# Two recurrent layers with routed experts on one core: GpSimd's scatters in blocks of eight that must land

## The chip, the cores and the metric

The kernel runs on one core of one Trainium2 chip. The metric is device time in microseconds (us) of one execution, as the median of several; less is better. The core has five engines that matter here: TensorE (PE), VectorE (DVE), ScalarE (ACT), GpSimd (POOL) and SyncE (SP). Each works through its own list of instructions in order and waits on semaphores for the others. SP, ACT and POOL also issue DMA transfers; all transfers of the core share 16 DMA engines.

## The reference, cut to what matters

The input is 4 sequences of 1024 tokens of 256 numbers in float32. Two layers follow, and each adds `s * silu(ffn(xn))` to `x`, where `xn` is the layer's normalised input. In layer 0 `s` is a gated recurrence, in layer 1 an attention over cosines. The part that the change touches is how tokens reach the experts of `ffn`:

```
xn = _layernorm(x, axis=-1)
topk_idx, topk_weight = _route(x, gate_weight, e_bias)      # 4 of 16 experts for each token
combine = (jax.nn.one_hot(topk_idx, E) * topk_weight[..., None]).sum(axis=1)
g = jnp.einsum('th,eih->tei', x, gate_proj)
u = jnp.einsum('th,eih->tei', x, up_proj)
act = jax.nn.silu(g) * u
expert_out = jnp.einsum('tei,ehi->teh', act, down_proj)
y = jnp.einsum('teh,te->th', expert_out, combine)
```

Layer 1 has 16 other experts, the same choice of 4, and a shared expert besides.

## The kernel before

**Routing by rows in DRAM.** The kernel computes only the chosen experts. DVE works out, for each token and each of its 4 choices, a row number in a DRAM table (`rows_in`), so that each expert's tokens stand together in tiles of 128 rows. GpSimd then scatters: one indirect DMA (L582, in `scattered`) takes 128 tokens (one column of a block of 512) and writes their 256 numbers to the 128 rows that one of the 4 choices names. A block of 512 tokens so takes 4 columns by 4 choices, 16 scatters.

**Groups.** Layer 0 has two groups of blocks (`HALVES`): three blocks (48 scatters) and five (80 scatters). Layer 1 has two groups of two sequences (`GROUPS`), four blocks or 64 scatters each. `dispatch` (L589) issues a group of layer 0; `dispatch1` (L934) one of layer 1, where GpSimd also loads each block from DRAM first (L949) and copies row information beside it (L950, L951).

**Experts.** `experts` (L596) walks over a group's rows in quads of 4 tiles: 16 and 24 quads in layer 0, 20 and 20 in layer 1. A quad is loaded three quads ahead (`load`, L621; by SP in layer 0, by ACT in layer 1), turned (L630), multiplied (L642), turned again (L659), multiplied (L667), and copied to a tile `o` by DVE (L685) and ACT (L679). There are three buffers of `xs` and three of `o`. Layer 0 stores `o` by rows (L717, ACT); layer 1 scatters it with four indirect DMAs of GpSimd per quad (L1203). Later, GpSimd gathers each token's four results of layer 0 (L724).

**What sets the order.** The program's generators are interleaved by hand with a model of time (`clock`, `pool_free`, the constants PAIR, INDIRECT and so on), and that fixes each engine's list of instructions. Waits are put in by the framework. GpSimd's DMAs take eight semaphores in turn, so that from the ninth on each scatter waits for the landing of the scatter eight before it.

Of the kernel before, what the change touches and what calls it, by code (L numbers as in the profile page):

```python
# [22 lines left out]
NS = TB // P  # L23
XB, GB, QB, OB = 8, 4, 3, 3
E, G = 16, 4
TOPK = 4
# [37 lines left out]
def two_layer_kernel(  # L64
# [18 lines left out]
    nc = tc.nc  # L83
# [488 lines left out]
    def indirect(n):  # L572

        pool_free[0] = max(pool_free[0], clock[0]) + n * INDIRECT
        return pool_free[0]

    def scattered(views, tokens, row, c0):

        indirect(len(views))
        for i, view in enumerate(views):  # L580
            s, k = divmod(i, TOPK)
            nc.gpsimd.indirect_dma_start(  # L582
                out=view,
                out_offset=bass.IndirectOffsetOnAxis(ap=row[:, c0 + s, k : k + 1], axis=0),
                in_=tokens[:, s, :],
                in_offset=None,
            )

    def dispatch(g, tokens, row):  # L589

        n = NS * TOPK
        views = dram_disjoint_views(rows_in[g], len(tokens) * n)
        for i, t in enumerate(tokens):
            scattered(views[i * n : (i + 1) * n], t, row, i * NS)

    def experts(groups, of_tiles, w_sb, we, hid, store, target=None, begin=None, end=None):  # L596

# [225 lines left out]
    def routed0(g, hs, lg):  # L823
        em, comb = yield from route(lg, len(HALVES[g]) * NS, r0b_sb, False)
        row, top, of_tile = yield from places(em, g, WE, "mm")
        dispatch(g, [hs[part] for part in HALVES[g]], row)
        with tc.issue_after(latest(mybir.EngineType.DVE)):
            w = all_of(weights_by_slot(normalized(comb), top, em, g))
        return row, w, of_tile
# [104 lines left out]
    def dispatch1(h):  # L934
        while not clearing.done:
            yield PIECE
        row, top, _ = placed1[h]
        pieces = [(b, q) for b in GROUPS[h] for q in range(NQ)]
        n = NS * TOPK
        views = dram_disjoint_views(rows_in[G1 + h], len(pieces) * n)  # L940

        tokens = {}
        for i in range(-AHEAD, len(pieces)):
            if i + AHEAD < len(pieces):
                j = i + AHEAD
                tokens[j] = t = xpool.tile([P, NS, D + INFO], F32, tag="x", name="t_half", bufs=XB)
                ts = slice(j * NS, (j + 1) * NS)
                b, q = pieces[j]
                nc.gpsimd.dma_start(out=t[:, :, 0:D], in_=block(normed, b, q))  # L949
                nc.gpsimd.tensor_copy(t[:, :, D : D + TOPK], top[:, ts, 0:TOPK])  # L950
                nc.gpsimd.tensor_copy(t[:, :, D + TOPK], result0[:, ts])  # L951
            if i >= 0:
                scattered(views[i * n : (i + 1) * n], tokens.pop(i), row, i * NS)
                while clock[0] < pool_free[0] - n * INDIRECT:
                    yield PIECE
        dispatched.add(h)
# [489 lines left out]
```

## Time and profile before

| | |
|---|---|
| three runs, median (least to most) | 1158.03 us (1157.47 to 1162.15) |
| the profiled execution's own time | 1148.62 us |
| its span, first to last instruction | 1146.9 us |
| mean granted TensorE clock in it | 0.952 |
| scatters of layer 0 (L582, from `x_half`) | 128, from 49.5 to 238.5 us, mean 1043 ns |
| scatters of layer 1 (L582, from `t_half`) | 128, from 633.4 to 806.5 us, mean 996 ns |

The profile is one execution, with times counted from its first instruction. "Busy" is time in instructions. The chain of waits follows the work that ended last back to the start. The timeline lists the instructions of an engine with the idle time in front of each and what ended it. "DMA to landing" is the time from a DMA's issue to the semaphore that tells that its data are written; for the scatters the profile has it for two of each eight, the fifth and sixth of layer 0's.

### The profile page before, as it was taken

The numbers are of one execution on the slowest core, as the hardware profiler recorded it, in microseconds if no ns is written. First come the engines' busy times: TensorE is split into PE (matmuls) and PEld (weight loads), VectorE is DVE, ScalarE is ACT, GpSimd is POOL, SyncE is SP. The second block draws the span as 40 slices with busy tenths as digits, with TensorE's granted clock in tenths as the row PEclk, the third lists the DMA queues.
The fourth block names the chain that finished last, engine by engine and source line by source line (L and its number), as shares of the span: only waits on it lengthen the run. The fifth ranks groups of instructions, "written<-read, shape, count | busy, mean of one in ns | idle before, by whom it ended". The sixth has DMA issues, their size and how long they took to land.

```text
span 1146.9 us, 16132 instructions
## 1 busy us (share of the span) xinstructions
PE 1032.5 (90%) x4928; PEld 765.6 (67%) x4928; DVE 650.2 (57%) x1963; ACT 467.2 (41%) x1030; POOL 565.0 (49%) x589
## 2 busy tenths in 40 slices
PE   5688699999889999888589999998899999999996
PEld 4255378887768788565357766765677777676665
DVE  4866953332786633167976973023633336776665
ACT  3345464444444544222143522221555555553132
POOL 1277377722760000377433777777446666776000
PEclk9868799999899999988699999999899999999999
DMA  8996569999998488977246533464545669994871
GB/s 346 396 407 253 181 204 319 328 286 274 299 302 242 134 235 243 320 189 185 84 137 243 208 122 139 140 213 139 196 163 184 188 197 353 359 337 140 273 238 37
DMA packets 118963, 264.81 MB, mean 231 GB/s; under 512 B 14177, under 2 KB 71649, under 8 KB 117601
## 3 DMA queue, kind: packets, MB, share of 16 engines
q1 hardware_dynamic: 77792, 137.18, 38.2%
q0 software_dynamic: 27264, 75.86, 19.6%
q10 hardware_dynamic: 13824, 50.75, 12.5%
q8 instruction: 43, 0.70, 0.3%
q14 instruction: 40, 0.32, 0.1%
HBM read 119.34 MB, written 144.39 MB: 230 GB/s over the span
## 4 chain that ended last, share of the span: by engine, by line
PE 65%; DVE 17%; DMA 8%; issue 4%; ACT 3%; POOL 2%; ACTq 0%; DVEq 0%; POOLq 0%
PE gu L642 14%; PE acc L667 11%; PE acc L1089 7%; PE tp L630 6%; PE gu L1136 4%; PE acc L1152 4%; PE mm L1057 4%; PE mm L1136 3%; DMA xs<-rows_in 3%; DMA r<-rows_out,row 3%; PE tp L659 3%; PE acc L296 2%; DVE x_half L1242 2%; PE mm L514 1%; DMA normed<-y 1%
## 5 line engine op out<-in xcount | busy, mean ns | idle before, releaser
L724 POOL DMA_INDIRECT r<-rows_out,row x128 | 131.4, 1027 | 240.9 <-DMA normed<-y 133.8
L642 PE MATMUL gu<-w_sb,xT 128*128 x1280 | 239.7, 331 | 0.5 <-issue 0.5
L642 PEld LDWEIGHTS gu<-w_sb,xT 128*128 128x128 f32 x1280 | 195.6, 193 | 14.6 <-issue 1.3
L1203 POOL DMA_INDIRECT results<-o,dest x160 | 159.7, 998 | 89.9 <-issue 28.2
L582 POOL DMA_INDIRECT rows_in<-x_half,row x128 | 133.5, 1043 | 101.6 <-issue 51.6
L667 PE MATMUL acc<-w_sb,hT 128*128 (+1 forms) x640 | 180.1, 397 | 2.5 <-ACT hT L661 2.4
L469 DVE SCALAR_TENSOR_TENSOR h<-sg,gu 128x256 f32<-128x256 f32 (+1 forms) x160 | 56.0, 351 | 166.9 <-ACT sg L468 166.5
L582 POOL DMA_INDIRECT rows_in<-t_half,row x128 | 127.5, 996 | 41.0 <-issue 39.0
L1089 PE MATMUL acc<-val,es 128*128 128x256 f32 x512 | 127.3, 393 | 6.3 <-ACT t L468 5.5
L634 ACT COPY xT<-tp 128x512 f32<-128x512 f32 x160 | 93.9, 587 | 91.0 <-PE tp L630 85.4
L667 PEld LDWEIGHTS acc<-w_sb,hT 128*128 128x128 f32 (+1 forms) x640 | 106.9, 189 | 30.2 <-issue 15.5
L1089 PEld LDWEIGHTS acc<-val,es 128*128 128x128 f32 x512 | 98.0, 198 | 31.1 <-issue 9.6
L630 PE MATMUL tp<-ident,xs 128*128 128x128 f32 x640 | 103.0, 285 | 11.8 <-DMA xs<-rows_in 11.8
L630 PEld LDWEIGHTS tp<-ident,xs 128*128 128x128 f32 x640 | 75.6, 144 | 46.3 <-issue 24.6
L468 ACT ACTIVATE sg<-gu 128x256 f32<-128x256 f32 (+1 forms) x160 | 52.9, 331 | 105.9 <-PE gu L642 101.1
L685 DVE COPY o<-acc 128x512 f32<-128x512 f32 x80 | 55.1, 688 | 63.4 <-PE acc L667 62.8
L659 PE MATMUL tp<-ident,h 128*128 128x128 f32 (+1 forms) x320 | 62.5, 277 | 13.4 <-DVE h L653 11.9
L1136 PE MATMUL mm<-xnT,w_sb 128*128 128x512 f32 x128 | 62.5, 611 | 11.6 <-DVE act L469 11.6
L1057 PE MATMUL mm<-projT 128*128 128x512 f32 (+3 forms) x192 | 70.4, 490 | 0.0
L661 ACT COPY hT<-tp 128x256 f32<-128x256 f32 (+1 forms) x160 | 58.5, 366 | 27.8 <-PE tp L659 26.2
L1136 PE MATMUL gu<-xnT,w_sb 128*128 128x512 f32 x128 | 60.5, 595 | 2.3 <-ACT val L1011 1.7
L1152 PEld LDWEIGHTS acc<-w_sb,act 128*128 128x128 f32 x256 | 48.2, 190 | 19.8 <-issue 9.7
(225 smaller groups left out, 1457.0 us busy)
## 6 DMA issues: line engine op xcount, KB each, us to landing
rows_in<-zeros SPq DMA_DIRECT2D x20, 1044.0 KB, 12.3
xs<-rows_in ACTq DMA_DIRECT2D x40, 522.0 KB, 5.4
xs<-rows_in SPq DMA_DIRECT2D x40, 512.0 KB, 6.1
rows_out<-o ACTq DMA_DIRECT2D x40, 512.0 KB, 7.0
r<-results SPq DMA_DIRECT2D x32, 512.0 KB, 6.1
rows_in<-zeros SPq DMA_DIRECT2D x1, 12288.0 KB
rows_in<-zeros SPq DMA_DIRECT2D x1, 8192.0 KB
w_sb<-in_w_dram SPq DMA_DIRECT2D x4, 1536.0 KB, 15.5
```

Of the source, the lines that this page charges most:

```text
L582: nc.gpsimd.indirect_dma_start(out=view, out_offset=bass.IndirectOffsetOnAxis(ap=row[:, c0 + s, k : k + 1], axis=0), in_=tokens[:, s, :], ...
L630: nc.tensor.transpose(tp[:, at : at + P], xs[:, j % per * 2 + i, kc * P : (kc + 1) * P], ident)
L634: nc.scalar.copy(xT.rearrange("p i k t -> p (i k t)"), tp)
L642: nc.tensor.matmul(ps[:, i * 2 * hid : (i + 1) * 2 * hid], lhsT=xT[:, i, kc, :], rhs=w_sb[:, bass.ds(off + kc * 2 * hid, 2 * hid)], start= ...
L659: nc.tensor.transpose(tp[0:hid, i * P : (i + 1) * P], h[:, i, :], ident)
L667: nc.tensor.matmul(ps[:, i * D : (i + 1) * D], lhsT=hT[0:hid, i * P : (i + 1) * P], rhs=w_sb[0:hid, bass.ds(expert(2 * j + i) + 4 * hid, D ...
L724: nc.gpsimd.indirect_dma_start(out=r[:, k, :], out_offset=None, in_=rows_out[g], in_offset=bass.IndirectOffsetOnAxis(ap=row[:, c, k : k + ...
L1057: nc.tensor.matmul(ps[:, at:TB], lhsT=projT[kc][:, t * P : (t + 1) * P], rhs=projT[kc][:, q * TB + at : (q + 1) * TB], start=(kc == 0), st ...
L1089: nc.tensor.matmul(av[s // 2][:, (s % 2) * D : (s % 2 + 1) * D], lhsT=es[:, s * P : (s + 1) * P], rhs=val[t // NS][:, t % NS, :], start=(t ...
L1136: nc.tensor.matmul(ps, lhsT=w[:, kc, j * P : (j + 1) * P], rhs=xr[:, kc, :], start=(kc == 0), stop=(kc == KC - 1),)
L1152: nc.tensor.matmul(ys[s // 2][:, (s % 2) * D : (s % 2 + 1) * D], lhsT=h[:, s * P : (s + 1) * P], rhs=ds1_sb[:, j, :], start=(j == 0 and s ...
L1203: nc.gpsimd.indirect_dma_start(out=views[g - G1][QUAD * q + i], out_offset=bass.IndirectOffsetOnAxis(ap=dest[:, i : i + 1], axis=0), in_=o ...
```

## The change

`scattered` gets an argument `landed`. When it is true, GpSimd writes a zero into the first element of two columns of the token tile after each eight scatters of those columns. The framework makes that memset wait until the eight DMAs that read the columns have landed. `dispatch` sets it for layer 0's second group alone; `dispatch1` leaves it at true, so both groups of layer 1 have it. The tile's contents are not read afterwards.

```diff
-    def scattered(views, tokens, row, c0):
+    def scattered(views, tokens, row, c0, landed=True):
...
             nc.gpsimd.indirect_dma_start(
...
             )
+            if landed and s % 2 and k == TOPK - 1:
+                nc.gpsimd.memset(tokens[:, s - 1 : s + 1, 0:1], 0.0)
...
-            scattered(views[i * n : (i + 1) * n], t, row, i * NS)
+            scattered(views[i * n : (i + 1) * n], t, row, i * NS, landed=g > 0)
```

Built, the changed kernel has the same list of instructions as before on PE, DVE, ACT and SP. GpSimd's list gains 26 memsets (10 in layer 0, 16 in layer 1). The framework places them later than the source does:

```
layer 0, second group:  12 scatters, memset, 8 scatters, memset, ... 8 scatters, memset, 4 scatters, memset
layer 1, each block:    12 scatters, memset (first eight), 4 scatters, memset (second eight)
```

In layer 0 the memset for a block of eight stands four scatters behind that block's last, except for the tenth, behind which come the gathers of L724. In layer 1 the memset of a token block's first eight stands four scatters behind them, and that of its second eight directly behind its last scatter; in the first token block of the first group that second memset stands one scatter later, behind the load of another block. The last memset of layer 1 stands in front of the first store of L1203.

## The prediction

> **What bounds the kernel.** First the page: its busy shares and the shares of the chain of waits.
>
> ```profile
> PE 1032.5 (90%) x4928; PEld 765.6 (67%) x4928; DVE 650.2 (57%) x1963; ACT 467.2 (41%) x1030; POOL 565.0 (49%) x589
> ...
> PE 65%; DVE 17%; DMA 8%; issue 4%; ACT 3%; POOL 2%; ACTq 0%; DVEq 0%; POOLq 0%
> ```
>
> PE is busy 90% of the span, GpSimd half of it, and GpSimd has 2% of the chain. So a later scatter costs time only where PE comes to wait for it. Next the page's groups, which give a scatter's price:
>
> ```profile
> L582 POOL DMA_INDIRECT rows_in<-x_half,row x128 | 133.5, 1043 | 101.6 <-issue 51.6 <-DVE ends L388 45.2 <-DMA rows_in<-x_half,row 1.8
> ...
> L582 POOL DMA_INDIRECT rows_in<-t_half,row x128 | 127.5, 996 | 41.0 <-issue 39.0 <-DMA rows_in<-t_half,row 1.5 <-POOL t_half L951 0.5
> ```
>
> A scatter takes about 1.0 us and 0.3 us of issue in front of it: the starts in the timeline are 1.27 us apart. The existing waits for the scatter eight before cost 1.8 and 1.5 us in all, because eight scatters last 10.2 us and a landing is shorter than that. What matters is how long landings take. The answer for L582 gives it by stretches of time (two samples of each eight): 182 to 187, 193 to 195, 203 to 206, 213 to 216, 224 to 227 and 234 to 237 us:
>
> ```profile
> DMA to landing us min/median/max: 8.0/8.2/8.4
> DMA to landing us min/median/max: 8.5/8.6/8.6
> DMA to landing us min/median/max: 5.2/5.7/6.3
> DMA to landing us min/median/max: 8.8/9.1/9.3
> DMA to landing us min/median/max: 4.2/4.7/5.2
> DMA to landing us min/median/max: 7.5/7.9/8.3
> ```
>
> From 130 to 182 us the samples run from 2.4 to 5.7 (median 3.2); in layer 1 they run from 2.4 to 3.7 up to 744 us (median 2.6), then 2.7 to 6.9 around 760, 2.4 to 2.9 from 768 to 800, and 6.8 to 7.5 at 802 to 804.
>
> Last, who needs the scatters of layer 0's second group. These are GpSimd's, SP's and PE's timelines around 240 us:
>
> ```profile
> 238.52 0.96 POOL L582 DMA_INDIRECT rows_in<-x_half,row  x1 [0.31 <-issue]
> 276.87 0.99 POOL L724 DMA_INDIRECT r<-rows_out,row  x1 [37.39 <-DMA xs<-rows_in]
> ```
> ```profile
> 233.49 0.32 SPq L621 DMA_DIRECT2D xs<-rows_in  x1
> 244.22 2.65 SPq L621 DMA_DIRECT2D xs<-rows_in  x2
> ```
> ```profile
> 255.67 0.60 PE L630 MATMUL tp<-ident,xs 128*128 128x128 f32 x4
> ```
>
> The last scatter starts at 238.52; SP's first load of the second group, released for it, goes at 244.22, so that scatter took 5.7 us to land. PE turns a quad in 6.5 us (the loads follow its releases at 233.49, 240.0, 246.55), and the load released at 240.0 is that of a quad three ahead: it is due at 255.67. The next load, at 246.55, landed in 5.9 us. With that, the first one landed at 250.1: **5.5 us of slack**. GpSimd itself has 37.4 us of idle time before its gathers.
>
> **The change, part by part.**
>
> *The memset itself.* Behind a scatter, a GpSimd instruction of another kind starts with no gap (L949 at 655.41, when the scatter before it ends), and the scatter after such an instruction starts 0.16 us behind it (L951 to L582 at 656.70) in place of 0.30. The small memsets of L165 and L171 take 89 ns. So a memset whose wait is over costs 0.09 + 0.16 - 0.30, about nothing, 26 times.
>
> *Layer 0.* Nine of ten memsets stand four scatters behind the block they wait for. From the start of a block's eighth scatter to the end of the twelfth is 4 x 1.27 + 0.96 = 6.0 us. The stall is the eighth's landing time less 6.0. The samples are of the fifth and sixth; in the last block the fifth took 8.3 and the eighth 5.7, so the eighth may be 2.6 below the fifth or as high as the median. Blocks with medians of 3.2, 5.7 and 4.7 cost nothing. Those with 8.2, 8.6 and 9.1 cost 2.2 + 2.6 + 3.1 = 7.9 at the most, and with 2.2 less (from the median) 0 + 0.4 + 0.9 = 1.3 at the least. I take 4.5: the last scatter starts at 243 and the load goes at about 248.7. The next load, due at 246.55, now goes right behind it, and the two share the DMA engines; a load under such traffic took 11.4 us at 233.49. With 7 us, between 5.9 and 11.4 and nearer to the quiet one since no scatter is left in flight, it lands at 255.7, when PE wants it. PE's stall is 0 by this and 7.9 us at worst (4.5 replaced by 7.9, landing in 11.4: 252.1 + 11.4 - 255.67 = 7.9). I put **0.5 us**. A stall here is not got back: PE's list is in order, the last quads of the first group stand behind the stalled turn, and the gathers at 276.87 wait for their stores.
>
> *Layer 1.* A token block's second memset stands right behind its last scatter and costs landing + 0.09 + 0.16 - 1.27 us: with 2.5 us 1.5. Seven stand in front of scatters or loads of GpSimd; the first has a load and a scatter between (over 2.5 us) and costs nothing. So 6 x 1.5 = 9.0, and 3 more for the one near 766 us, where the landing was 5 to 6: 12 us. Who needs them? The second group's rows are loaded from the 21st quad on, far later (a quad takes 5.8 us from 847 us on, and the first starts at 805). But the stores of L1203 are queued behind:
>
> ```profile
> 806.47 0.96 POOL L582 DMA_INDIRECT rows_in<-t_half,row  x1 [0.30 <-issue]
> 814.27 0.96 POOL L1203 DMA_INDIRECT results<-o,dest  x1 [6.84 <-DVE h L469]
> ```
> ```profile
> 833.64 0.69 DVE L685 COPY o<-acc 128x512 f32<-128x512 f32 x1 [2.53 <-PE acc L667]
> ```
>
> There are 6.84 us of idle time. The first store now goes at 806.47 + 12 + 2.4 to 7.5 + 0.25 = 821 to 826, which is 7 to 12 us late. Four stores of a quad take 5.1 us; GpSimd falls behind and catches up at the fifth quad (its first store was at 847.29; stores from 824 on are done with four quads at 844). The buffer of `o` that binds is the first, wanted by the fourth quad's copy at 833.64: its stores start until 821 + 3.8 or 826 + 3.8, and land in 2.4 to 6.2 us (rows of L1203 from 814 to 842), so at 827 to 836. The stall is 0 to 2.4 us; I take **1 us**, above the quiet end because the landings of the scatters at 802 to 804 were slow.
>
> *A rule weighed.* The Trainium skill ("DMA: Bandwidth & Descriptors", section "Anatomy of one DMA — SWDGE (gpsimd) path") prices a DMA issued by GpSimd at about 2.0 us plus its bytes over 436 thousand per us, nearly all of it waiting for the write's receipt; an estimate from it is 2.3 us for a scatter of 131,072 bytes. The trace's least is 2.4, but 8 to 9 us stand in layer 0, so it holds only on quiet DMA engines. By the rule no block of layer 0 stalls, and the sum would be 0 us; by the rows it is the sum below.
>
> *Sum.* 0.5 + 1 = 1.5 us: the profiled execution's 1148.62 (span 1146.9 and 1.7 around it) becomes 1150.1. The three runs' median lies 9.4 above the profiled execution; added to it, 1158.03 + 1.5 gives **1159.5 us**.
>
> **The rivals.** About 0.5% (5.8 us) is what a measurement of this kernel can tell from no change.
>
> *Nothing that can be measured (0.70).* For it: the four scatters in front of each memset in layer 0, the 5.5 us of slack, the 6.84 us before the first store. It has two forms: the waits bite but are covered (1159.5), or they hardly bite, as the waits for eight before already hold GpSimd to eight in flight (1158.0).
>
> *Slower: layer 0's rows come late (0.23).* The mechanism is the one load at 244.22. From the point where the scatters' delay plus the load's longer landing pass 5.5 us, each further us is a us of PE. For it: DMA engines are full there (8 to 9 us landings, one load of 11.4). With the upper bounds it is 7.9, with the 2.4 of layer 1 10.3: 1168.3. If the fifth and seventh blocks also slipped over 6.0 us it would be a few us more. Against it: a GpSimd that waits sends less, which shortens the landings.
>
> *Faster: fewer scatters in flight leave the DMA engines to others (0.07).* PE waits for transfers while scatters run in one place alone, 6.5 us at 799 to 805.5, for a load that landed in 5.1; the least for such a load is 3.8, so 1.3 us is to be won, 1156.7. The other waits come after the scatters have ended (6.33 us of PE at 284, behind the gathers). To pass 5.8 us more would have to change than any row shows.
>
> **How the numbers follow.** The likeliest is the first, 1159.5. The range goes down to 1154, the faster rival less the 2 to 3 us by which runs differ, and up to 1169, the slower rival's sum. Slower by over 0.5% has 0.23, faster by over 0.5% 0.05 (0.02 of the third rival's 0.07 stays within), within it 0.72.
>
> **What would show it.** Memsets of under 0.2 us, with idle time in front of three of layer 0's and nearly none at the others, say the landings are as I read them; the last scatter of layer 0 near 243 and SP's load near 249, and no wait of PE for `xs` at 256, say the slack held. In layer 1 the second memsets should have 1.5 us of idle time, the last scatter start near 818, the first store at 821 to 826, and DVE's copy of `o` at the fourth quad wait little. A wait of PE at 256 of more than 5 us, or one at 834, makes the prediction wrong; so does any block of layer 0 that waits for its landing from the block's own end, which would give 2 to 7 us for each of ten.

## The result, and the profile after

| | before | changed |
|---|---|---|
| median of 14 runs each, on one chip (least to most) | 1157.79 us (1153.37 to 1162.15) | 1164.58 us (1158.83 to 1172.38) |
| ratio to before, 95% interval | | 1.0058 (1.0034 to 1.0081) |
| the profiled execution, its span | 1148.62, 1146.9 us | 1161.13, 1159.4 us |
| first and last scatter of layer 0's second group | 132.07, 238.52 us | 132.71, 255.41 us |
| SP's first load of that group | 244.22 us | 258.02 us |
| PE turns that quad | 255.67 us | 261.85 us |
| first store of layer 1 (L1203, now L1207) | 814.27 us | 836.26 us |

The kernel is 0.58% slower, 6.8 us in the medians. Line numbers behind the change are 4 higher, and the memset is L591. The page of the changed kernel again has the busy shares and the shares of the chain of waits:

```profile
PE 1037.4 (89%) x4928; PEld 770.6 (66%) x4928; DVE 650.1 (56%) x1963; ACT 467.2 (40%) x1030; POOL 566.2 (49%) x615
...
PE 59%; DVE 15%; DMA 11%; POOL 6%; issue 5%; ACT 3%; ACTq 0%; SPq 0%; POOLq 0%; DVEq 0%
```

The work is as before; DMA rose from 8% to 11% of the chain and GpSimd from 2% to 6%. From 228 to 258 us the chain, which before ran on PE there, now goes through the scatters of layer 0's second group, 18.4 us of it through their landings; the larger part of GpSimd's growth is its gathers (L728, 4%), from 285 us on. GpSimd's timeline at the end of that group shows how the scatters came there (start, duration, instruction, and in brackets the idle time in front of it and what ended it):

```profile
235.80 0.96 POOL L583 DMA_INDIRECT rows_in<-x_half,row  x1 [0.30 <-issue]
240.82 0.10 POOL L591 MEMSET x_half<- 128x2 f32 x1 [4.06 <-DMA rows_in<-x_half,row]
241.49 0.97 POOL L583 DMA_INDIRECT rows_in<-x_half,row  x1 [0.56 <-issue]
...
251.31 0.12 POOL L591 MEMSET x_half<- 128x2 f32 x1
251.61 0.97 POOL L583 DMA_INDIRECT rows_in<-x_half,row  x1 [0.19 <-issue]
...
255.41 0.96 POOL L583 DMA_INDIRECT rows_in<-x_half,row  x1 [0.30 <-issue]
257.94 0.10 POOL L591 MEMSET x_half<- 128x2 f32 x1 [1.58 <-DMA rows_in<-x_half,row]
284.99 0.99 POOL L728 DMA_INDIRECT r<-rows_out,row  x1 [26.94 <-DMA g_half<-hidden_rows]
```

The memset at 240.82 waits 4.06 us for its block although four further scatters stand between; the one at 251.31 waits for nothing. The answer for L591 sums up all ten memsets of layer 0:

```profile
  DMA rows_in<-x_half,row: 16.2, 5
```

Four memsets inside the group wait, for blocks 4, 5, 7 and 8: 3.54 + 4.56 + 2.49 + 4.06 = 14.65 us; 1.58 us is the tenth, behind the last scatter. From the start of a block's eighth scatter to the end of the wait those four took 9.6, 10.6, 9.5 and 10.1 us; the others had landed by the time that the four scatters behind them were issued (6.0 to 7.1 us). SP's timeline shows what those four have in common:

```profile
174.73 0.43 SPq L843 DMA_DIRECT2D rows_in<-zeros  x1
...
188.26 0.43 SPq L843 DMA_DIRECT2D rows_in<-zeros  x1
...
207.92 1.95 SPq L843 DMA_DIRECT2D rows_in<-zeros  x1
...
227.42 0.43 SPq L843 DMA_DIRECT2D rows_in<-zeros  x1
```

These are clears of about 1 MB each, by which SP zeroes rows for layer 1 (`cleared`, L839 before). The profile has the landing of two of them, at 188.26 and 207.92: 16.4 and 15.9 us from issue. The eighth scatters of the blocks that waited start at 177.49, 191.53, 216.73 and 230.73, each 3 to 9 us behind a clear; that of block 6 starts at 206.59, just ahead of one, and those of blocks 9 and 10 at 245.28 and 255.41, 18 and 28 us behind the last one, which at 16 us had landed.

SP issued the same clears before the change, too:

```profile
174.85 0.43 SPq L839 DMA_DIRECT2D rows_in<-zeros  x1
...
188.37 0.44 SPq L839 DMA_DIRECT2D rows_in<-zeros  x1
...
207.87 1.41 SPq L839 DMA_DIRECT2D rows_in<-zeros  x1
...
227.37 0.44 SPq L839 DMA_DIRECT2D rows_in<-zeros  x1
```

Set against them, the prediction's samples of landing from 182 us on fall into two groups: the eight scatters that started 5 to 9 us behind one of these clears took 7.5 to 9.3 us, the four that started 15 to 18 us behind one took 4.2 to 6.3.

So the last scatter is late. PE's timeline shows the price:

```profile
254.89 1.03 PE L671 MATMUL acc<-w_sb,hT 128*128 x4
261.85 1.09 PE L634 MATMUL tp<-ident,xs 128*128 128x128 f32 x4 [5.92 <-DMA xs<-rows_in]
```

PE stands still for 5.92 us where before it turned at once. Matched one by one, PE's 4928 instructions start within 0.1 us of the times of before just ahead of this turn, 6.2 us later at it, 7.8 from 257.6 to 284 (times of before), 9.1 at 290, 10 to 12 from 359 to 522, 13 to 17 from 537 to 567, and 12.5 to 13.0 from 568 us to the end. The step from 6.2 to 7.8 is PE's clock: for the 3.45 us behind the wait the granted clock is 0.53, where before it was 1.00.

Layer 1, GpSimd's timeline again:

```profile
835.59 0.10 POOL L591 MEMSET t_half<- 128x2 f32 x1 [2.23 <-DMA rows_in<-t_half,row]
836.26 0.97 POOL L1207 DMA_INDIRECT results<-o,dest  x1 [0.57 <-DVE projT L181]
...
859.91 0.96 POOL L1207 DMA_INDIRECT results<-o,dest  x1 [3.23 <-DVE h L469]
```

The first store is 22.0 us later than before, 9.1 more than the 12.9 by which PE is late there. GpSimd has caught up at 859.91, where it waits for DVE again. PE never waited for it: between 640 and 910 us its only long wait is the 6.2 us for `xs` that was there before, and its lateness stays between 12.6 and 13.0.

### The profile page after: what moved, and what is told of

Same layout as the page of the kernel before. It is cut to its first block, busy times and chain, and to the rows that moved or that the text cites. A ratio compares the mean times of both kernels' runs of the same rounds, so it can differ in the third digit from the quotient of the medians.

```text
span 1159.4 us, 16205 instructions
## 1 busy us (share of the span) xinstructions
PE 1037.4 (89%) x4928; PEld 770.6 (66%) x4928; DVE 650.1 (56%) x1963; ACT 467.2 (40%) x1030; POOL 566.2 (49%) x615
## 3 DMA queue, kind: packets, MB, share of 16 engines
q10 hardware_dynamic: 13824, 50.75, 12.6%
## 4 chain that ended last, share of the span: by engine, by line
PE 59%; DVE 15%; DMA 11%; POOL 6%; issue 5%; ACT 3%; ACTq 0%; SPq 0%; POOLq 0%; DVEq 0%
PE gu L646 11%; PE acc L671 9%; PE acc L1093 7%; PE tp L634 5%; POOL r L728 4%; PE gu L1140 4%; PE acc L1156 4%; PE mm L1061 4%; PE mm L1140 3%; DMA xs<-rows_in 3%; DMA r<-rows_out,row 2%; PE tp L663 2%; PE acc L296 2%; DVE x_half L1246 2%; DMA rows_in<-x_half,row 2%
## 5 line engine op out<-in xcount | busy, mean ns | idle before, releaser
L728 POOL DMA_INDIRECT r<-rows_out,row x128 | 130.7, 1021 | 236.2 <-DMA g_half<-in_x_dram 137.1
L646 PE MATMUL gu<-w_sb,xT 128*128 x1280 | 242.6, 333 | 0.5 <-issue 0.4
L1207 POOL DMA_INDIRECT results<-o,dest x160 | 159.2, 995 | 74.6 <-issue 29.7
L1093 PEld LDWEIGHTS acc<-val,es 128*128 128x128 f32 x512 | 97.8, 198 | 32.0 <-issue 10.1
L1156 PE MATMUL acc<-w_sb,act 128*128 128x256 f32 x256 | 61.2, 387 | 6.2 <-DVE act L1150 6.2
## 6 DMA issues: line engine op xcount, KB each, us to landing
rows_in<-zeros SPq DMA_DIRECT2D x20, 1044.0 KB, 16.1
w_sb<-in_w_dram SPq DMA_DIRECT2D x4, 1536.0 KB, 16.9
```

What stands on the lines that cost most here:

```text
L646: nc.tensor.matmul(ps[:, i * 2 * hid : (i + 1) * 2 * hid], lhsT=xT[:, i, kc, :], rhs=w_sb[:, bass.ds(off + kc * 2 * hid, 2 * hid)], start= ...
L728: nc.gpsimd.indirect_dma_start(out=r[:, k, :], out_offset=None, in_=rows_out[g], in_offset=bass.IndirectOffsetOnAxis(ap=row[:, c, k : k + ...
L1093: nc.tensor.matmul(av[s // 2][:, (s % 2) * D : (s % 2 + 1) * D], lhsT=es[:, s * P : (s + 1) * P], rhs=val[t // NS][:, t % NS, :], start=(t ...
L1156: nc.tensor.matmul(ys[s // 2][:, (s % 2) * D : (s % 2 + 1) * D], lhsT=h[:, s * P : (s + 1) * P], rhs=ds1_sb[:, j, :], start=(j == 0 and s ...
L1207: nc.gpsimd.indirect_dma_start(out=views[g - G1][QUAD * q + i], out_offset=bass.IndirectOffsetOnAxis(ap=dest[:, i : i + 1], axis=0), in_=o ...
```

## The experiments

**What was to be told apart.** The theory after the result: the rows of layer 0's second group come late, since scatters behind a clear land slowly, and PE waits for them. The rivals: layer 1's late stores cost the time; the memsets themselves do; or the landings are slow whatever SP clears.

One thing must be known to read the ratios: of the four sets of runs only one (e9) fell on a chip as quick as that of the result; on the chips of the other three the kernel before itself takes 1471 to 1496 us, and their traces hold no landing times for the scatters.

**e9: the changed kernel, with the clears moved behind the second group's scatters.** The generators that issue the clears wait first, and then come at a shorter pace:

```diff
+        yield 130.0
...
-                yield CLEAR
+                yield 11.0
```

> The changed kernel with SP's clears of rows_in (1 MB each) moved behind the scatters of layer 0's second group, on another chip, since the first chip's traces were of a program that was held up elsewhere and its memsets in layer 0 never had to wait. Theory 'clears': the scatters' slow landings (9 to 10.6 us for the eighth of a block) come from sharing the DMA engines with the clears; without them the memsets of layer 0's second group wait under 2 us in all, the last scatter starts near 240 us, PE does not wait for xs at 256, and the time is that of before or up to 0.5% better. Rival 'other traffic': loads, stores and gathers are enough; the memsets still wait 10 to 15 us in all, the last scatter starts at 250 to 255 and the ratio to before stays near 1.006.

("The first chip" there is one of the slower ones.) Measured: 1146.85 us (8 runs) against 1152.21 of the kernel before (13 runs): ratio 0.9936 (0.9911 to 0.9962). The answer for L591, which had 16.2 us in five waits:

```profile
  PE gu L646: 1.6, 1
  DMA rows_in<-x_half,row: 1.2, 2
```

The 1.6 is the tenth memset's wait, put down to a neighbour. Two memsets inside the group still wait, 0.34 and 0.89 us, and the samples of landing between 180 and 240 us lie at 2.8 to 6.6 us. The last scatter starts at 238.90, and SP's first load goes at 241.5. PE's timeline at the turn that had waited 5.92 us:

```profile
254.47 1.03 PE L671 MATMUL acc<-w_sb,hT 128*128 x4
255.33 0.60 PE L634 MATMUL tp<-ident,xs 128*128 128x128 f32 x4
```

No idle time. The stretch from 180 to 260 us, in the view by windows (length, busy time and count of PE, PEld, DVE, ACT and POOL, clock, DMA share, GB/s), of before, of the changed kernel and of e9:

```profile
180.00:260.00 80.00, 80.00 (x444) 69.92 (x444) 28.25 (x62) 36.91 (x88) 44.28 (x46) 1.00 1.00 309
```
```profile
180.00:260.00 80.00, 75.92 (x418) 65.85 (x416) 27.40 (x60) 34.66 (x83) 45.95 (x54) 0.99 0.93 280
```
```profile
180.00:260.00 80.00, 80.00 (x445) 69.99 (x444) 28.21 (x62) 36.89 (x88) 44.96 (x53) 1.00 0.74 241
```

Before, the DMA engines were full (share 1.00) without harm to PE, since nothing there waited for a scatter but the ninth after it and, at the end, SP's load, which had 5.5 us of slack. With the same ten memsets and the clears gone the share is 0.74, and PE is busy throughout. The theory holds: without the clears the same scatters land in time, so it is the clears, beside the other traffic, that made the landings slow, and the landings that made the group late. The bound on the waits was 2 us in all and 2.8 was found, and the gain of 0.64% is a little over the 0.5% allowed; the rest is as expected. This version is quicker than the kernel before; the changed kernel wasn't run on this chip, and only its ratio of 1.0058 on its own can be set beside the 0.9936. e9 keeps all 26 memsets and layer 1's waits (1.6 to 2.6 us at each of the seven second memsets that wait), so these can cost at most what the clears' move gains by itself. How much that is, without memsets, is open: the run for it (e10) fell on one of the slower chips.

**On the other chips.** There the whole schedule is different: in e1 the second group's scatters end at 278 us and SP's first load of it goes at 364, some 85 us later, so they press on nobody. In e4 and e12 the load does follow the last scatter closely (2.6 and 4.4 us behind its start), but PE turns that quad 10.8 and 7.7 us after the load's issue without a wait for it. These runs can't price the lateness in layer 0. They show something else.

*e1, blocks in layer 0 alone* (`landed=False` in `dispatch1`).

> The wait for blocks is kept in layer 0's second group and taken out of both groups of layer 1. Theory 'late rows': the whole loss comes from layer 0, where the last scatter of the second group started 16 us later than before and PE stood 5.9 us at the first load of that group; so this kernel is as slow as the changed one, about 1.006 of before (1.004 to 1.008), with the last scatter of layer 0 starting near 255 us. Rival 'late stores': the loss comes from layer 1, whose first store of results went 22 us later; then this kernel equals before within 0.2%. If both pay, it lies at about 1.003.

Measured: 1488.73 against 1496.22, ratio 0.9938 (0.9901 to 0.9974). Nine of the ten memsets wait 0.00 us and the last 1.59. Neither theory's: there was no wait to cost anything.

*e2 and e11, blocks in layer 1 alone* (`landed=False` in `dispatch`), on two chips.

> The wait for blocks is kept in both groups of layer 1 and taken out of layer 0. 'Late rows': no loss, 1.000 (0.998 to 1.002), last scatter of layer 0 near 238.5 us, no wait of PE for the first load of the second group; layer 1's scatters end 12 to 16 us later against PE's own instructions and PE does not wait for it. 'Late stores': all of the loss is here, about 1.006.

> The blocks and their memsets in layer 1 alone. Theory 'late rows of layer 0': layer 1's waits cost PE nothing; its scatters end some 9 us later and the first store of layer 1's results goes some 9 us later than before, no PE wait for it, ratio 0.998 to 1.002. Rival 'late stores': the buffer o comes free late and the loss is here: ratio 1.004 or more, with a wait of DVE or ACT for o and of PE for acc around 830 us.

Measured: ratios 0.9681 (0.9627 to 0.9734) and 0.9716 (0.9633 to 0.9798). Both theories had 1.00 or more. The loss of the rival isn't there, but nor is the equality that the other foresaw.

*e3, e4 and e12: no wait for a landing, but 2 (e3) or 8 (e4, e12) memsets of a scratch tile between the blocks of layer 0's second group*, with the scatters held in order; layer 1 as before.

```diff
+            if landed and s % 2 and k == TOPK - 1:
+                for _ in range(8):
+                    with tc.issue_after(latest(mybir.EngineType.Pool)):
+                        nc.gpsimd.memset(scratch, 0.0)
```

> No wait for landings at all: between the blocks of eight scatters of layer 0's second group GpSimd does two memsets of a scratch tile (128x200), which puts its last scatter some 3 to 5 us later; layer 1 as before. 'Late rows' with the 5.5 us of slack that the prediction read: no loss, 1.000 (0.998 to 1.002), PE does not wait for the first load of the second group. If the slack is not there, 1.003 to 1.004. 'Late stores': 1.000.

> As the kernel with the short delay, with eight memsets between blocks: the last scatter of layer 0's second group starts some 16 to 20 us later, without any wait for a landing. 'Late rows': a late scatter costs the same whatever made it late, so 16 to 20 less 5.5 to 7.6 us of slack, or 9 to 14 us, 1.008 to 1.012, and PE waits so long for the first load of the second group. 'Late stores', or a cost that lies in the waits or in the fewer scatters in flight and not in the lateness: 1.000.

> In layer 0's second group GpSimd does eight memsets of a scratch tile (0.32 us each, 2.6 us) between its blocks of eight, in order, and never waits for a block's landing; layer 1 as before. The last scatter of the group starts some 21 to 24 us later than before, near 260. Theory 'late rows of layer 0': lateness alone is the price, so SP's first load of the second group goes near 264 and PE waits 10 to 15 us for xs there; ratio 1.006 to 1.013. Rival 'landing wait itself' (the wait does harm beyond its lateness): no loss, 0.998 to 1.003.

Measured: 0.9815 (0.9769 to 0.9861) with 2, 0.9604 (0.9558 to 0.965) and 0.9584 (0.9542 to 0.9626) with 8. The scatters do end later (the last starts at 304.75 us in e12), and the kernel is 4% quicker, against every theory.

*e7, one small memset behind each eight in both layers, no wait for a landing.*

> The 26 memsets stand directly behind each eight scatters in GpSimd's list, in layer 0's second group and in layer 1, but write a scratch tile, so that they wait for no landing. If the instructions themselves cost, it is as slow as the changed kernel, 1.006; if it is the wait, it equals before, 1.000 (0.998 to 1.002), and the last scatters of both layers start within 1 us of before.

Measured: 1.0039 (1.0004 to 1.0073). Each memset takes 0.11 us, and the next scatter starts 0.19 us behind it: no pause, and no gain either. As to what the memsets cost, the interval holds the 1.006 of the one theory and reaches into the 0.998 to 1.002 of the other, so it decides nothing.

*e5 and e10: the kernel before with the late clears; e6: the changed one with them.*

> The kernel before, with the twenty transfers of 1 MB of zeros that clear layer 1's tables (SP) begun only behind the scatters of layer 0's second group (the first near 265 us in place of 118), and then closer together; no wait for blocks. Theory 'clears': these transfers make the scatters' landings of 8 to 10 us; so the samples of landing between 182 and 240 us fall from 8 to 9 to under 5 us. Rival 'other traffic': PE's loads and stores of quads make them, and they stay at 8 or more. The time itself may move either way by 1% as the clears now share the DMA engines with the gathers; it is the base for the next kernel.

> The kernel before (no memsets) with SP's clears behind the scatters of layer 0's second group. Theory 'clears': the samples of scatter landing between 182 and 240 us fall from 8 to 9 us to 6.5 or less, the last scatter starts near 238, and the gain of the version with blocks (0.9936 of before) is the clears' alone: ratio 0.990 to 0.997 here too, within 3 us of the version with blocks. Rival 'blocks gain': pauses of GpSimd help other transfers, so without them the gain is gone: 0.998 to 1.002.

> The changed kernel with the clears begun late in the same way. 'Clears': the memsets of layer 0 hardly wait (under 2 us in all in place of 14.7), the last scatter starts at most 3 us after that of the kernel with late clears alone, PE does not wait for the first load of the second group, and the time equals that kernel's within 0.2%. 'Other traffic': the memsets wait 10 to 15 us again and it is 0.5% slower than that kernel.

Measured: 0.9993 (0.9952 to 1.0035) and 1.0012 (0.9981 to 1.0044) without blocks, 0.9704 (0.9649 to 0.9759) with them. Landings can't be read there, so "clears" and "other traffic" aren't told apart by these.

*e8: the kernel before, once more, for its trace.*

> The kernel before, for a second profile. The profiled execution of before took 1148.62 us while its other runs lie between 1153.37 and 1162.15; that of the changed kernel 1161.13, 12.5 us more, while the medians differ by 6.8. If the first profile was an uncommonly quick execution, this one takes 1153 to 1160 us, the last scatter of layer 0 still starts near 238.5 us, and the extra time lies in stretches that the change does not touch, behind 290 us.

Measured: 1464.55 us, one run. The expectation missed: it took the chip to be like the first.

**What these runs have in common.** The view by windows, from 179 to 283 us, first of e10 (GpSimd scatters without a pause), then of e12 (some 2.7 us more between blocks of eight):

```profile
179.00:283.00 104.00, 41.11 (x100) 21.97 (x100) 19.25 (x39) 12.56 (x21) 79.92 (x80) 0.61 0.32 115
```
```profile
179.00:283.00 104.00, 91.95 (x443) 71.91 (x444) 41.48 (x85) 44.83 (x97) 79.62 (x127) 0.96 0.76 237
```

GpSimd is busy for the same 80 us in both, yet PE does 100 matmuls in one and 443 in the other, and ACT 21 instructions against 97. The DMA engines are at 0.32 in e10, so it isn't that they are full. PE's timeline of e10 in that stretch:

```profile
241.25 0.69 PE L659 MATMUL tp<-ident,h 128*128 128x128 f32 x2 [22.56 <-ACT hT L661]
...
293.80 0.69 PE L659 MATMUL tp<-ident,h 128*128 128x128 f32 x2 [11.78 <-ACT hT L661]
```

PE waits for ACT, and ACT for something that the trace doesn't show; the chain of waits puts 18% of e10's span down to an unknown queue, and nothing of before's. On the result's chip nothing of the kind is seen: from 188 to 239 us, while GpSimd scatters, PE is busy for all of the 51 us.

So on those chips the other engines hardly advance while GpSimd issues indirect DMAs back to back, and each pause lets them on. The gains go with the pauses: none in e7 and in e5 and e10; 0.75 us more between blocks in e3, 1.9%; 2.7 us in e4 and e12, 4%; 12 us of waits spread over layer 1 in e2 and e11, 3%, and e11's lead over e10, PE instruction by PE instruction, reaches 61 us while its layer 1 scatters run (27 are left at the end). The 0.6% of e1, which has no pause, fits no such order and stays unexplained. That the pauses bring it is shown by e3 and e4, which wait for no landing, hold the scatters in the same order and differ in the length of the pause alone: 1.9% against 4.0%. What holds the engines back there isn't shown. The changed kernel itself wasn't run there; e6, which has its blocks and late clears, is at 0.9704.

## Why the prediction was right in the time and wrong in the path

The time, 1164.58 us, lies in the range, 5.1 above the forecast, but only because the slower rival's sum set the upper end: the likeliest case, no change beyond 5.8 us, missed. It is the rival "layer 0's rows come late" that happened, so by its own test (a wait of PE at 256 of more than 5 us) the prediction was wrong in its path.

- **The memset itself, about nothing:** right where it didn't wait (0.12 us, next scatter 0.19 behind). Where it did, the next scatter started 0.56 behind it instead of the 0.16 assumed: 0.10 + 0.56 - 0.30 = 0.36 us, four times, 1.4 us that the sum lacked.
- **Layer 0, 4.5 us late, 7.9 at the most:** this step failed. The last scatter was 255.41 - 238.52 = 16.9 us later, 16.2 without the 0.64 by which the group began late; the waits and the gaps behind them give 14.65 + 1.4 = 16.1. Four blocks took 9.5 to 10.6 us to land, not three at most 9.1. The step took the fifth and sixth scatter's landing as the most that the eighth could have, and put the eighth lower still, from the last block, where the fifth started 7 us behind a clear and the eighth 11. It read samples by time without asking what transfer lay beside each. So blocks 4 and 7, with samples of 3.4 to 3.5 and 5.2 to 6.3, were taken to cost nothing: their fifth and sixth scatters started ahead of a clear or 15 us behind one, their eighths (176.34 and 217.27 before) 1.5 and 9 us behind one.
- **"A GpSimd that waits sends less, which shortens the landings":** wrong. 0.07 of DMA share fell away (1.00 to 0.93), and the eighths' landings behind a clear, 9.5 to 10.6 us, were longer than the samples before, at most 9.3. The rule of the Trainium skill that was weighed ("DMA: Bandwidth & Descriptors", "Anatomy of one DMA — SWDGE (gpsimd) path": about 2.0 us and the bytes) holds, with an estimate of 2.3 us, only for quiet stretches: 2.4 us is the least in e9, 10.6 the most measured behind a clear.
- **Slack of 5.5 us, PE's stall 0.5:** the slack's working was right. SP's load went 13.8 us later, and with no scatter in flight it landed in 3.8 us instead of 5.9, not in the 7 that was taken. 13.8 - 5.5 - 2.1 = 6.2, which is PE's lateness at that turn. That each further us is a us of PE left out the clock behind the wait, which brought 1.6 more. The 7.8 in all is close to the 7.9 of the upper bounds by luck: those had the scatters 7.9 us late and the load landing in 11.4, and the runs showed 16.9 and 3.8.
- **Layer 1, stores 7 to 12 us late, PE's stall 1 (0 to 2.4):** right. They were 9.1 us late, the seven second memsets that waited did so for 1.6 to 2.2 us each, two of the others for 0.6 and 0.1, and PE lost 0.
- **The sum, 1.5 us:** 6.8 in the medians. The 7.8 us by which PE is late behind the one load covers it; the sum had 0.5 for that. The two profiled executions differ by 12.5, and so does PE at its last instruction, but that of before is quicker than each of its 14 timed runs, so it isn't settled how much of the 4.7 us that came later (among them 7.6 us of waiting behind the gathers instead of 6.3, 6.8 instead of 5.5 around 490) belongs to the change.

No run on the two quicker chips took layer 0 and layer 1 apart, or delayed the scatters without a landing; that the loss is layer 0's rests on the trace of the changed kernel and on e9.

## What to carry to other kernels

Before a wait for a landing is added, look up which large transfer of any other queue is under way at each sample of that landing: the landings that were not sampled behaved here like those beside the same transfer, and an average over a stretch hides them. The cheapest cure of a wait that bites may be on another queue: moving clears that nobody needed yet took the loss back and, on e9's chip, left the kernel 0.6% under the one before. And a change that shifts one engine's pauses is to be timed on more than one chip.

## What the runs showed of the hardware that was not expected

- From 174 to 240 us, a clear of 1 MB on SP's queue (16 us from issue to landing in the changed kernel) goes with slower landings of the 128 KB scatters on GpSimd's queue: 7.5 to 10.6 us for those sampled or waited for 1 to 9 us behind a clear, in before and in the changed kernel, against 2.8 to 6.9 in e9, without clears. An earlier clear of before, at 145.69, landed in 9.6 us, and the two samples behind it took only 5.7 and 4.6 us.
- A wait of PE costs more than its length: behind the 5.92 us the granted clock was 0.53 for 3.45 us, which added 1.6 us.
- The kernel before took 1152 to 1158 us in the sets of runs of the result and of e9, and 1471 to 1496 on the three chips of the other sets. Of the 316 us between the profiled executions of before and e8, the same kernel, PE is busy for 61 (1093.2 against 1032.5), at a mean granted clock of 0.855 against 0.952; the rest is waiting, 69 us of it from 174 to 280 us alone, where GpSimd scatters and PE is busy for 37.4 us instead of 106.
